# Two graph layers on one core: the first layer's adjacency product by Strassen's scheme, in step with the projection before it, and sums moved to GpSimd at the end

## The chip, the cores and the metric

The kernel runs on one core of one Trainium2 chip. The metric is the device time of one execution in microseconds (us). Before the change its median over 10 runs is 2680.24 us, with single runs between 2676.88 and 2682.38 us.

A core has five engines that each work through a queue of their own: TensorE (PE in the profile; its weight loads are shown apart, as PEld), VectorE (DVE), ScalarE (ACT), GpSimd (POOL) and SyncE (SP, which here only issues transfers). They meet at semaphores.

## The reference

The input x holds 64 batches of 256 tokens with 512 features; adj is one 256 by 256 matrix for all batches. Two layers follow each other, each with a layer norm and a relu ahead and a residual sum behind:

```python
h = relu(layernorm(x))
x = x + (einsum('nm,bmd->bnd', adj, h) @ W0 + b0)          # layer 0
h = relu(layernorm(x))
q, k, v = (h @ W + b for W, b in ...)                       # layer 1: 8 heads of 64
scores = q k^T / 8 + (1 - adj) * -1e9
x = x + (softmax(scores) v) @ Wo + bo
```

All of it is in float32. The change is about the einsum with adj in layer 0, and about the last groups of layer 1.

## The kernel before

**Groups.** The batches are worked in 32 groups of two. The first layer runs over all groups; its results (the residual and the normalised, transposed features, called hidden) go to DRAM and are read again by the second layer, which also runs group by group.

**A group of the first layer** (`ready` at line 678, `layer0` at line 702). A group has four token tiles of 128 tokens. DVE takes the mean and variance of each tile (`moments`, lines 42 and 43), then `norm_scales` (lines 46 to 54) writes rs and nb: two small operations on DVE (lines 51, 52) and two on POOL (lines 53, 54: a power and a product). ACT then writes the normalised relu, h (line 693). TensorE multiplies h as the weights with the transposed adjacency as the moving operand: 16 matmuls of 128 by 128 by 256 (line 714), which leave y transposed, yT, in four PSUM banks that ACT copies to SBUF (line 724). 

**Strassen's scheme** is used already for every projection. `project` (line 456) works a product of 2 by 2 blocks with 7 block products instead of 8, in the form of Winograd. It needs four sums of weight blocks (s1 to s4, made once) and four sums of data blocks (t1 to t4, `Halves.sums`, line 446, on POOL). Each block product is four matmuls of 128 by 128 by 256 (line 453). Partial sums stay in PSUM where they can, and are added to their place in SBUF by DVE (`add`, line 665). Two of the banks start with the bias, copied there by ACT (`seeded`, line 255). The second layer applies the scheme a second time to three of the seven block products (`project2`, line 564, matmuls of 128 by 128 by 128).

Behind the first layer's projection DVE takes the statistics of the new x (lines 761 and 766), `norm_scales` follows for each batch, ACT writes the relu (line 741), DVE transposes it by blocks of 32 (line 747), and SP stores residual (line 751) and hidden (line 756).

**What sets the order.** Nothing is scheduled by a planner: each engine runs its instructions in the order in which the program issues them. The program issues by steps: generators yield after a block product, `tick` (line 271) then advances a clock by one and issues whatever `after(delay, ...)` (line 267) has put off until that step. So the delays in the calls of `ready`, in `relu`, `turn`, `leave_residual` and `leave_hidden`, and in `score` and `attend` set where each instruction stands in its engine's queue. Each group of the first layer is 11 steps: four for the adjacency, seven for the projection. PSUM banks are handed out first in, first out (`bank`, `give`).

**The second layer** has per group and per half of the heads: `score` (line 888: matmuls of line 898, mask by DVE at line 904, a subtraction on POOL at line 910 or on DVE at line 908, the exponential on ACT at line 915, key sums on POOL at line 922), `attend` (line 924: sums of line 931, products with v of line 938, reciprocals on DVE at line 951, the division at line 969), and the projections q, k, v and o. At the division, `HO[g].sums` makes the data sums of the output projection, and `note` (line 963) lets ACT add up the reciprocals for a check of the softmax's range: at the very end a flag is set from these sums (lines 1078 to 1082), and a general path for inputs out of range is run if it is above zero.

Of the kernel before, what the change touches and what calls it, by code (L numbers as in the profile page):

```python
# [8 lines left out]
F32 = mybir.dt.float32  # L9
I32 = mybir.dt.int32  # L10
AF = mybir.ActivationFunctionType
ALU = mybir.AluOpType
# [186 lines left out]
def kernel(  # L199
# [499 lines left out]
                after(scales_at[t // n], scales, t // n)  # L699
            after(relus_at[t], relu, t)  # L700

    def layer0(g):

        xt, h = X.pop(g), H0.pop(g)

        yT = act.tile([P, DC, GN], F32, tag=f"yT{g % 2}", name=f"yT_{g}")
        halves = Halves(f"y_{g}", [yT[:, :, k * N:(k + 1) * N] for k in range(GB)], g % 2 if g < NG - 1 else 0)
        pss = {}

        def adjacency(d, b):  # L710
            if d not in pss:
                pss[d] = bank([P, GN], f"py_{g}_{d}")
            for k in range(NT):
                nc.tensor.matmul(pss[d][:, b * N:(b + 1) * N], h[:, b * NT + k, d * P:(d + 1) * P],  # L714
                                 adjT[:, k, :], start=(b + k == 0), stop=(k == NT - 1), skip_group_check=True)

        if g == 0:
            for d in range(DC):
                adjacency(d, 0)
        for d in range(DC):  # L720
            for b in range(1 if g == 0 else 0, GB):
                adjacency(d, b)
            ps = pss.pop(d)
            nc.scalar.copy(yT[:, d, :], ps)  # L724
            give(ps)
            halves.sums(nc.gpsimd, ("t1",) if d < 2 else ("t2",), d % 2)
            if d == 3:
                halves.sums(nc.gpsimd, ("t3", "t4"))
            if d == 2:
                seeds = seeded(b0_r, f"w_{g}")  # L730
            yield

        mv = small.tile([P, T, 2], F32, tag="mv", name=f"mv1_{g}")
        st = [small.tile([P, 2, nc.vector.BN_STATS_DIM], F32, tag="st1", name=f"st1_{g}_{t}", bufs=8) for t in range(T)]
        h1 = act.tile([P, T, D], F32, tag="h1", name=f"h1_{g}")
        r = act.tile([P, DC * NI, GB, NT, 32], F32, tag="r", name=f"r_{g}")
        done = []

        def relu(k, rs, nb):
            for t in range(NT):  # L740
                nc.scalar.activation(h1[:, k * NT + t, :], xt[:, k * NT + t, :], AF.Relu,  # L741
                                     bias=nb[:, t:t + 1], scale=rs[:, t:t + 1])

        def turn(k):

            for t in range(NT):
                nc.vector.transpose(r[:, :, k, t, :], h1[:, k * NT + t, :].rearrange("p (j b) -> p j b", b=32))

        def leave_residual(k):
            for i in range(NI):  # L750
                nc.sync.dma_start(by_block(X1[g][k], i), blocks_of(xt, i, k))

        def leave_hidden():
            dst = HT[g].rearrange("(j f) d i k n -> i f d j (k n)", f=32)
            for i in range(NI):
                nc.sync.dma_start(dst[i], r[32 * i:32 * i + 32].rearrange("p (d j) k t b -> p d j (k t b)", j=NI))

        def finished(i, k):
            o = quarter(xt, i, k)
            for t in range(NT):  # L760
                nc.vector.bn_stats(st[k * NT + t][:, i, :], o[:, t, :])  # L761
            done.append(k)
            if done.count(k) == 2:
                s = slice(k * NT, (k + 1) * NT)
                for t in range(k * NT, (k + 1) * NT):
                    nc.vector.bn_aggr(mv[:, t, :], st[t])
                rs, nb = norm_scales(nc, small, mhalf, mv[:, s, :], f"1_{g}_{k}")
                wait = 2 if g < NG - 1 else 3
                after(wait, relu, k, rs, nb)
                after(1 if len(done) < 4 else 2, leave_residual, k)  # L770
                after(wait + 1, turn, k)
# [152 lines left out]
    def attend(g, qd):  # L924


        pd = bank([P, GN], f"pden_{g}_{qd}")
        po = [bank([P, GN], f"pav_{g}_{qd}_{f}") for f in range(2)]
        for b in range(GB):
            for h in range(4):  # L930
                nc.tensor.matmul(pd[h * 32:(h + 1) * 32, b * N:(b + 1) * N], ones[:, 0:32], AS[h // 2, b][:, h % 2, :],  # L931
                                 start=(b == 0), stop=True, tile_position=(0, h * 32), skip_group_check=True)
        for b in range(GB):
            v = V[g][qd, b]
            for k in range(NT):
# [12 lines left out]
        give(pd)  # L948

        def invert(c):  # L950
            nc.vector.reciprocal(rden[:, c * P:(c + 1) * P], den[:, c * P:(c + 1) * P])  # L951

        early = 2 if g >= FIRST2 and (g, qd) != (NG - 1, 1) else 4
        for c in range(early):
            invert(c)
        if qd == 0:

            last = g == NG - 1
            OT[g] = (xpool if last else act).tile([P, DC, GN], F32, tag="x" if last else "r", name=f"oT_{g}")
            HO[g] = Halves(f"o_{g}", [OT[g][:, :, k * N:(k + 1) * N] for k in range(GB)], 0 if last else 1)  # L960

        def note():
            nc.scalar.activation(den, rden, AF.Identity, accum_out=stats[:, 1, i:i + 1])

        def divide():
            for c in range(early, 4):
                invert(c)
            for f in range(2):
                nc.vector.tensor_tensor(OT[g][:, 2 * qd + f, :], po[f], rden, op=ALU.mult)
                give(po[f])  # L970
            if g < NG - 1:
                after(3, note)
            else:
                note()
            eng = nc.gpsimd if g < NG - 2 else nc.vector
            if qd == 0:
                HO[g].sums(eng, ("t1",))
            else:
                HO[g].sums(eng, ("t3", "t2", "t4"))
                if g >= FIRST2:  # L980
                    block_outputs(g, eng if g == NG - 1 else nc.gpsimd, 8 if g == NG - 2 else 2)

        after(1, divide)

# [5 lines left out]

    side = [[] for _ in range(NG)]
    mask_steps, bias_steps = masks(), out_bias()
    STEPS = 11
    for i, n in enumerate("qkvo"):
        side[2 + 2 * i].append((load_layer1, n))
        side[4 + 4 * i].append((lambda n: weight_sums(nc.gpsimd, L1[n][0], n, [2 + STEPS * j for j in range(4)]), n))
# [4 lines left out]

    ready(0, (0, 0, 2, 2), (0, 2), (1, 1, 3, 3), batches=2)
    load(1)
    tick()
    turn_adjacency()
    split_bias(b0_r)
    tick()
    weight_sums(nc.vector, w0_sb, "0", (0, 0, 6, 7))
    load(2)
    tick()  # L1010
    tick()
    for g in range(NG):
        for fn, *args in side[g]:
            fn(*args)

        if g == 0:
            ready(1, (1, 2, 3, 4), (5,), (6, 7, 8, 9))
            ready(2, (8, 8, 10, 11), (12,), (16, 17, 18, 19))
        elif g + 2 < NG:
            ready(g + 2, (1, 4, 7, 8), (9,), (16, 17, 18, 19))  # L1020
        if g == NG - 2:
            hidden_sums(0, 1, 2, 12, 16)
        steps = layer0(g)
        run(steps, 4)
        if g + 3 < NG:
            load(g + 3)
        if g == NG - 3:
            load_hidden(0)
        if g == NG - 1:
            load_hidden(1)  # L1030
            break
        run(steps)
    run(queries_keys(0))
    score(0, 0, 12)
    tick()
    run(steps)
    hidden_sums(1, 1, 2, 6, 7)
# [1 line left out]
    for g in range(NG):  # L1039
# [13 lines left out]
        if g + 1 < NG:  # L1053
            run(queries_keys(g + 1))
        else:
            last = post(g - 1, seed_outputs(g - 1))
            run(last, 5)
        attend(g, 1)
        if g + 1 < NG:
            score(g + 1, 0, 5)  # L1060
# [5 lines left out]
            if g + 2 < NG:  # L1066
# [1 line left out]
                if g + 2 >= FIRST2:  # L1068
                    block_hidden(g + 2, 6)
                run(post(g, seeds))  # L1070
    tick()
    run(last)
    last = post(NG - 1, seed_outputs(NG - 1))
    run(last, 6)

    bad = tmp.tile([P, 2 * NG * HQ], F32, tag="u", name="bad")
    worst = small.tile([P, 1], F32, tag="worst", name="worst", bufs=1)
# [41 lines left out]
```

## Time and profile before

| | before |
|---|---|
| median of 10 runs | 2680.24 us |
| the profiled execution | 2678.61 us, span 2676.8 us |
| mean granted TensorE clock | 0.997 |
| PE busy | 2644.3 us |
| PEld busy | 2280.0 us |
| DVE busy | 1858.3 us |
| ACT busy | 964.7 us |
| POOL busy | 1780.2 us |
| HBM | 106.96 MB read, 100.66 MB written |

The span is the time from the first to the last instruction of the profiled execution. "Busy" is the time in which an engine had at least one instruction in work; overlapping instructions count once. In the timelines each line has the start and the length in us, the engine, the line in the program, the operation, output and inputs, shapes, and how many instructions were merged into the line (x8); a bracket at the end tells how long the engine sat idle before it, and what ended that. A float32 matmul of the program leaves two records of PE in the trace. The lines of a window give, for a stretch of time, the busy time of PE, PEld, DVE, ACT and POOL in this order, then the granted clock, the share of the DMA engines and the rate in GB/s.

The first layer fills the first 640 us, the second layer the rest; the last 77 us hold 55.77 us of PE.

### The profile page before, as it was taken

How to read it: one execution, taken by the hardware profiler on the slowest of the kernel's cores; microseconds unless marked ns; L12 is line 12 of the kernel's file. 1: busy time of each engine (PE TensorE's matmuls, PEld its weight loads, DVE VectorE, ACT ScalarE, POOL GpSimd, SP SyncE). 2: the span in 40 equal slices, each digit the busy share in tenths (PEclk: the TensorE clock that was granted, in tenths of full speed). 3: DMA queues.
4: the chain of work that ended last, by engine and by line, in shares of the span. 5: the costliest groups of instructions: out<-in, count | busy, mean ns of one | idle time of the engine just before them, and what ended most of it. 6: DMA issues, size and time to landing. Idle time of an engine off the chain costs nothing. (4 is left out here: it accounts for less than half of the span.)

```text
span 2676.8 us, 50183 instructions
## 1 busy us (share of the span) xinstructions
PE 2644.3 (99%) x19332; PEld 2280.0 (85%) x19332; DVE 1858.3 (69%) x4103; ACT 964.7 (36%) x1875; POOL 1780.2 (67%) x1568
## 2 busy tenths in 40 slices
PE   8999999999999999999999999999999999999997
PEld 7888888888888888888888888888888888888885
DVE  6777777774467766667677676676776666767776
ACT  4444445453333333333333333333333333333331
POOL 3454544444778777777777777777777777777772
PEclk9999999999999999999999999999999999999998
DMA  7776666663122211111111111112221111111110
GB/s 184 187 197 168 156 170 165 171 162 80 47 64 56 57 48 48 48 48 48 48 49 48 48 48 48 48 50 65 68 58 48 48 48 48 49 48 48 48 48 33
DMA packets 281058, 210.93 MB, mean 79 GB/s; under 512 B 145904, under 2 KB 212976, under 8 KB 280816
## 3 DMA queue, kind: packets, MB, share of 16 engines
q1 hardware_dynamic: 280352, 207.15, 29.9%
q8 instruction: 155, 2.54, 0.4%
q14 instruction: 87, 0.71, 0.1%
q10 hardware_dynamic: 464, 0.52, 0.1%
HBM read 106.96 MB, written 100.66 MB: 78 GB/s over the span
## 5 line engine op out<-in xcount | busy, mean ns | idle before, releaser
L910 POOL TENSOR_TENSOR a<-a,top 128x1024 f32<-128x1024 f32 x254 | 592.7, 2367 | 493.5 <-DVE a L904 493.5
L904 DVE SCALAR_TENSOR_TENSOR a<-sc,maskT 128x512 f32<-128x512 f32 x512 | 311.9, 680 | 122.0 <-PE sc L898 122.0
L922 POOL TENSOR_TENSOR as<-a 128x512 f32<-128x512 f32 x256 | 318.9, 1277 | 9.4 <-ACT a L915 8.4
L915 ACT ACTIVATE a<-a 128x1024 f32<-128x1024 f32 x256 | 270.7, 1058 | 10.1 <-POOL a L910 7.7
L53 POOL TENSOR_TENSOR rs<-rs,mhalf 128x2 f32<-128x2 f32 (+1 forms) x97 | 78.4, 808 | 268.0 <-DVE nb L52 267.8
L951 DVE RECIPROCAL rest<-rest 128x128 f32<-128x128 f32 x256 | 224.3, 919 | 34.9 <-ACT rest L947 34.9
L898 PE MATMUL sc<-q,k 64*128 64x256 f32 x2048 | 238.4, 383 | 0.0
L938 PE MATMUL pav<-a,v 128*32 128x256 f32 x4096 | 234.0, 379 | 0.0
L898 PEld LDWEIGHTS sc<-q,k 64*128 64x128 f32 x2048 | 194.2, 187 | 44.7 <-issue 26.3
L714 PE MATMUL py<-adjT,h 128*128 128x256 f32 x1024 | 228.2, 381 | 0.9 <-DVE adjT L333 0.9
L714 PEld LDWEIGHTS py<-adjT,h 128*128 128x128 f32 x1024 | 195.7, 191 | 28.5 <-ACT h L693 1.2
L938 PEld LDWEIGHTS pav<-a,v 128*32 128x32 f32 x4096 | 134.0, 110 | 87.5
L741 ACT ACTIVATE h<-x,nb,rs 128x512 f32<-128x512 f32 x128 | 97.1, 806 | 307.1 <-POOL nb L54 307.1
L947 ACT ACTIVATE rest<-pden 128x512 f32<-128x512 f32 x64 | 38.2, 597 | 414.7 <-PE pden L931 414.7
L665 DVE TENSOR_TENSOR k<-k,k 128x128 f32<-128x128 f32 (+1 forms) x300 | 96.0, 352 | 126.2 <-PE k L564 124.1
L446 POOL TENSOR_TENSOR t_y<-yT 128x256 f32<-128x256 f32 (+1 forms) x96 | 87.6, 913 | 45.1 <-ACT yT L724 41.7
L665 DVE TENSOR_TENSOR x<-o,x 128x128 f32<-128x128 f32 (+1 forms) x360 | 110.9, 349 | 3.1
L665 DVE TENSOR_TENSOR v<-v,v 128x128 f32<-128x128 f32 (+1 forms) x300 | 95.3, 351 | 14.5 <-PE v L564 11.5
L665 DVE TENSOR_TENSOR q<-q,q 128x128 f32<-128x128 f32 (+1 forms) x300 | 96.0, 352 | 13.6 <-PE q L564 11.5
L761 DVE BATCH_NORM_STATS2 st<-x 128x6 f32<-128x256 f32 x256 | 96.4, 418 | 4.4
L693 ACT ACTIVATE h<-x,nb,rs 128x512 f32<-128x512 f32 x128 | 93.9, 805 | 10.2 <-POOL nb L54 10.2
L446 POOL TENSOR_TENSOR t_y<-yT,t_y 128x256 f32<-128x256 f32 (+1 forms) x96 | 87.2, 916 | 13.3 <-ACT yT L724 13.3
(4280 smaller groups left out, 6494.5 us busy)
## 6 DMA issues: line engine op xcount, KB each, us to landing
x<-in_x_dram SPq DMA_DIRECT2D x256, 128.0 KB, 3.3
residual<-x SPq DMA_DIRECT2D x256, 128.0 KB, 2.3
hidden<-r SPq DMA_DIRECT2D x128, 256.0 KB, 4.7
h1T<-hidden SPq DMA_DIRECT2D x64, 512.0 KB, 9.6
x<-residual SPq DMA_DIRECT2D x32, 1024.0 KB, 7.5
out_dram<-x SPq DMA_DIRECT2D x62, 512.0 KB, 4.1
w_sb<-in_L_gnn_weight_dram SPq DMA_DIRECT2D x1, 1024.0 KB, 7.0
wq_sb<-in_L_gnn_Wq_dram SPq DMA_DIRECT2D x1, 1024.0 KB, 7.6
```

Source lines behind the costliest of these rows:

```text
L446: eng.tensor_tensor(self.t[n][:, c, :], self.operand(p, c), self.operand(q, c), op=ALU.subtract)
L665: nc.vector.tensor_tensor(o, ps, u, op=ALU.add)
L714: nc.tensor.matmul(pss[d][:, b * N:(b + 1) * N], h[:, b * NT + k, d * P:(d + 1) * P], adjT[:, k, :], start=(b + k == 0), stop=(k == NT - 1 ...
L741: nc.scalar.activation(h1[:, k * NT + t, :], xt[:, k * NT + t, :], AF.Relu, bias=nb[:, t:t + 1], scale=rs[:, t:t + 1])
L761: nc.vector.bn_stats(st[k * NT + t][:, i, :], o[:, t, :])
L898: nc.tensor.matmul(ps[j][:, kt * N:(kt + 1) * N], k[j * HD:(j + 1) * HD, c, kt * P:(kt + 1) * P], q[j * HD:(j + 1) * HD, c, :], start=(kt ...
L904: nc.vector.scalar_tensor_tensor(a[:, j * NT:(j + 1) * NT, :].rearrange("p k n -> p (k n)"), ps[j], SCALE, maskT_f, op0=ALU.mult, op1=ALU.add)
L910: nc.gpsimd.tensor_tensor(a, a, top_b, op=ALU.subtract)
L915: nc.scalar.activation(a, a, AF.Exp)
L922: nc.gpsimd.tensor_tensor(AS[c, b], a4[:, :, 0, :], a4[:, :, 1, :], op=ALU.add)
L938: nc.tensor.matmul(po[f][h * 32:(h + 1) * 32, b * N:(b + 1) * N], v[:, k, h * HD + f * 32:h * HD + f * 32 + 32], A[h // 2, b][:, (h % 2) * ...
L951: nc.vector.reciprocal(rden[:, c * P:(c + 1) * P], den[:, c * P:(c + 1) * P])
```

## The change

**Adjacency.** For groups 1 to 31 the product with adj is done by Strassen's scheme too, with one level: 7 block products, each of four matmuls of 128 by 128 by 128 (28 per group instead of 16 of twice the width). The blocks of adj are 128 by 128; their four sums are made once, on POOL (`adjacency_sums`). The blocks of h are halves of the features by token tiles; their four sums are made for every group on POOL (`feature_sums`, `last_feature_sum`). Three banks are used: four results are copied to yT by ACT, three are added to it by DVE. Group 0 keeps the old product (`first_adjacency`).

**Order.** The adjacency product of group g + 1 is issued between the block products of group g's projection, so that a group is 7 steps, not 11. The statistics, scales and relus of group g + 2, the sums, the load of group g + 3 and the weight sums get new steps. The last group's projection begins ahead of the second layer's first q and k, with four of its seven block products, and the hidden sums of group 0 stand next to it.

**The end of the kernel.** The data sums of the last two output projections are issued on POOL instead of DVE, those of group 30 seven steps later; the sum of reciprocals of the last group (`note`) is issued two or three steps later; the output projection of group 30 does a sixth of its seven steps ahead of the last attention; the flag is set behind two steps of the last projection instead of six.

```diff
-    def layer0(g):
-        ...
-        def adjacency(d, b):
-            ...
-                nc.tensor.matmul(pss[d][:, b * N:(b + 1) * N], h[:, b * NT + k, d * P:(d + 1) * P],
-                                 adjT[:, k, :], start=(b + k == 0), stop=(k == NT - 1), skip_group_check=True)
-        ...
+    def feature_sums(g):
+
+        def block(i, j):
+            return H0[g].rearrange("p (b j) d -> p b j d", b=GB)[:, :, j - 1, (i - 1) * HF:i * HF]
+        s12 = act.tile([P, 2, GB, HF], F32, tag="t2", name=f"hs12_{g}")
+        s4 = act.tile([P, GB, HF], F32, tag="t24", name=f"hs4_{g}")
+        HS[g] = dict(a11=block(1, 1), a12=block(1, 2), a22=block(2, 2), s1=s12[:, 0], s2=s12[:, 1], s3=block(2, 1), s4=s4)
+        for o, p, q, op in ((s12[:, 0], block(2, 1), block(2, 2), ALU.add), (s12[:, 1], s12[:, 0], block(1, 1), ALU.subtract),
+                            (block(2, 1), block(1, 1), block(2, 1), ALU.subtract)):
+            nc.gpsimd.tensor_tensor(o, p, q, op=op)
+
+    def last_feature_sum(g):
+        nc.gpsimd.tensor_tensor(HS[g]["s4"], HS[g]["a12"], HS[g]["s2"], op=ALU.subtract)
+
+    def adjacency(g):
+        ...
+        def product(ps, a, b, start=True):
+            for c in range(2):
+                for m in range(GB):
+                    nc.tensor.matmul(ps[:, c, m, :], HS[g][a][:, m, c * P:(c + 1) * P], AT[b],
+                                     start=(start and c + m == 0), stop=True, skip_group_check=True)
+        ...
+        pa = new("a")
+        product(pa, "a11", "b11")
+        nc.scalar.copy(place(0, 0), pa)
+        yield
+        pc = new("c")
+        product(pc, "s3", "t3")
+        nc.scalar.copy(place(1, 1), pc)
+        yield
+        product(pa, "s2", "t2", False)
+        nc.scalar.copy(place(1, 0), pa)
+        yield
+        pb = new("b")
+        product(pb, "a12", "b21")
+        more(pb, 0, 0)
+        give(pb)
+        yield
+        product(pa, "s1", "t1", False)
+        more(pa, 1, 1)
+        yield
+        product(pc, "a22", "t4", False)
+        more(pc, 1, 0)
+        give(pc)
+        yield
+        product(pa, "s4", "b22", False)
+        nc.scalar.copy(place(0, 1), pa)
+        give(pa)
+        after(1, YH[g].sums, nc.gpsimd, ("t1", "t2"))
+        after(2, YH[g].sums, nc.gpsimd, ("t3", "t4"))
+        yield
...
-            if g < NG - 1:
-                after(3, note)
-            else:
-                note()
-            eng = nc.gpsimd if g < NG - 2 else nc.vector
-            ...
+            after(2 if (g, qd) == (NG - 1, 1) else 3, note)
+            wait = 7 if (g, qd) == (NG - 2, 1) else 0
+            sums = lambda: HO[g].sums(nc.gpsimd, ("t3", "t2", "t4") if qd else ("t1",))
+            if wait:
+                after(wait, sums)
+            else:
+                sums()
+            if qd and g >= FIRST2:
+                block_outputs(g, nc.gpsimd, wait + 1 if g >= NG - 2 else 2)
...
+    ready(1, (4, 4, 4, 4), (4,), (5, 5, 6, 6))
+    after(6, feature_sums, 1)
+    after(7, last_feature_sum, 1)
...
-        elif g + 2 < NG:
-            ready(g + 2, (1, 4, 7, 8), (9,), (16, 17, 18, 19))
...
+        if g + 2 < NG:
+            ready(g + 2, (1, 1, 2, 2), (2,), (3, 3, 4, 4))
+            after(4, feature_sums, g + 2)
+            after(6, last_feature_sum, g + 2)
+        weighted, turned = layer0(g, seeds), adjacency(g + 1)
+        for i, n in enumerate((0, 0, 0, 1, 1, 2, 3) if g == 0 else (1, 1, 2, 2, 1, 0, 0)):
+            next(weighted)
+            for _ in range(n):
+                next(turned)
+            if i == 5:
+                seeds = seeded(b0_r, f"w_{g + 1}")
+            tick()
+            if i == 3 and g + 3 < NG:
+                load(g + 3)
...
+    hidden_sums(0, 1, 1, 2, 2)
+    steps = layer0(NG - 1, seeds)
+    run(steps, 4)
     run(queries_keys(0))
-    score(0, 0, 12)
+    score(0, 0, 6)
...
-            run(last, 5)
+            run(last, 6)
...
-    tick()
     run(last)
     last = post(NG - 1, seed_outputs(NG - 1))
-    run(last, 6)
+    run(last, 2)
```

More of the change, by code (lines that the diff above doesn't have):

```diff
@@ L700, in ready, with begin_y, first_adjacency, part @@
             after(relus_at[t], relu, t)
-    def layer0(g):
-        xt, h = X.pop(g), H0.pop(g)
-        yT = act.tile([P, DC, GN], F32, tag=f"yT{g % 2}", name=f"yT_{g}")
-        halves = Halves(f"y_{g}", [yT[:, :, k * N:(k + 1) * N] for k in range(GB)], g % 2 if g < NG - 1 else 0)
+    Y, YH, HS, AT = {}, {}, {}, {}
+    def begin_y(g):
+        yT = Y[g] = act.tile([P, DC, GN], F32, tag=f"yT{g % 2}", name=f"yT_{g}")
+        YH[g] = Halves(f"y_{g}", [yT[:, :, k * N:(k + 1) * N] for k in range(GB)], (g + 1) % 2)
+        return yT
+    def first_adjacency():
+        yT, h = begin_y(0), H0.pop(0)
         pss = {}
-        def adjacency(d, b):
+        def part(d, b):
             if d not in pss:
-                pss[d] = bank([P, GN], f"py_{g}_{d}")
+                pss[d] = bank([P, GN], f"py_{d}")
             for k in range(NT):
@@ L715, in adjacency @@
                                  adjT[:, k, :], start=(b + k == 0), stop=(k == NT - 1), skip_group_check=True)
-        if g == 0:
-            for d in range(DC):
-                adjacency(d, 0)
         for d in range(DC):
-            for b in range(1 if g == 0 else 0, GB):
-                adjacency(d, b)
+            part(d, 0)
+        for d in range(DC):
+            part(d, 1)
             ps = pss.pop(d)
@@ L725, in layer0, with adjacency_sums, block @@
             give(ps)
-            halves.sums(nc.gpsimd, ("t1",) if d < 2 else ("t2",), d % 2)
+            YH[0].sums(nc.gpsimd, ("t1",) if d < 2 else ("t2",), d % 2)
             if d == 3:
-                halves.sums(nc.gpsimd, ("t3", "t4"))
-            if d == 2:
-                seeds = seeded(b0_r, f"w_{g}")
+                YH[0].sums(nc.gpsimd, ("t3", "t4"))
             yield
+    def adjacency_sums():
+        def block(j, k):
+            return adjT[:, j - 1, (k - 1) * P:k * P]
+        t = act.tile([P, 4, P], F32, tag="t24o", name="adjT_t")
+        AT.update(b11=block(1, 1), b21=block(2, 1), b22=block(2, 2), t1=t[:, 0, :], t2=t[:, 1, :], t3=t[:, 2, :],
+                  t4=t[:, 3, :])
+        for o, p, q in (("t1", block(1, 2), block(1, 1)), ("t2", block(2, 2), AT["t1"]),
+                        ("t3", block(2, 2), block(1, 2)), ("t4", block(2, 1), AT["t2"])):
+            nc.gpsimd.tensor_tensor(AT[o], p, q, op=ALU.subtract)
@@ new lines, in last_feature_sum, with place, new, more @@
+    def last_feature_sum(g):
+        nc.gpsimd.tensor_tensor(HS[g]["s4"], HS[g]["a12"], HS[g]["s2"], op=ALU.subtract)
+    def adjacency(g):
+        yT = begin_y(g)
+        H0.pop(g)
+        def place(i, k):
+            return yT[:, 2 * i:2 * i + 2, :].rearrange("p c (b k n) -> p c b k n", b=GB, k=NT)[:, :, :, k, :]
+        def product(ps, a, b, start=True):
[3 more added lines that the diff above has]
+                                     start=(start and c + m == 0), stop=True, skip_group_check=True)
+        def new(n):
+            return bank([P, 2, GB, P], f"py_{g}{n}")
+        def more(ps, i, k):
+            o = place(i, k)
+            add(o, ps, o)
+        pa = new("a")
[27 more added lines that the diff above has]
+        yield
@@ L733, in layer0 @@
+    def layer0(g, seeds):
+        xt, halves = X.pop(g), YH.pop(g)
         mv = small.tile([P, T, 2], F32, tag="mv", name=f"mv1_{g}")
@@ L970, in divide @@
                 give(po[f])
-            if g < NG - 1:
-                after(3, note)
-            else:
-                note()
-            eng = nc.gpsimd if g < NG - 2 else nc.vector
-            if qd == 0:
-                HO[g].sums(eng, ("t1",))
-            else:
-                HO[g].sums(eng, ("t3", "t2", "t4"))
-                if g >= FIRST2:
-                    block_outputs(g, eng if g == NG - 1 else nc.gpsimd, 8 if g == NG - 2 else 2)
+            after(2 if (g, qd) == (NG - 1, 1) else 3, note)
[3 more added lines that the diff above has]
+                after(wait, sums)
+            else:
+                sums()
+            if qd and g >= FIRST2:
+                block_outputs(g, nc.gpsimd, wait + 1 if g >= NG - 2 else 2)
         after(1, divide)
@@ L992 @@
     mask_steps, bias_steps = masks(), out_bias()
-    STEPS = 11
+    STEPS = 7
     for i, n in enumerate("qkvo"):
@@ L1003 @@
     load(1)
+    ready(1, (4, 4, 4, 4), (4,), (5, 5, 6, 6))
+    after(6, feature_sums, 1)
+    after(7, last_feature_sum, 1)
     tick()
     turn_adjacency()
+    adjacency_sums()
     split_bias(b0_r)
@@ L1011 @@
     tick()
-    for g in range(NG):
+    steps = first_adjacency()
+    run(steps, 3)
+    seeds = seeded(b0_r, "w_0")
+    run(steps)
+    for g in range(NG - 1):
         for fn, *args in side[g]:
             fn(*args)
-        if g == 0:
-            ready(1, (1, 2, 3, 4), (5,), (6, 7, 8, 9))
-            ready(2, (8, 8, 10, 11), (12,), (16, 17, 18, 19))
-        elif g + 2 < NG:
-            ready(g + 2, (1, 4, 7, 8), (9,), (16, 17, 18, 19))
[L1021 to L1026, printed above, removed]
+        if g + 2 < NG:
[12 more added lines that the diff above has]
+                load(g + 3)
+        for rest in (weighted, turned):
+            for _ in rest:
+                pass
         if g == NG - 3:
             load_hidden(0)
[L1029 to L1032, printed above, removed]
+    load_hidden(1)
+    hidden_sums(0, 1, 1, 2, 2)
+    steps = layer0(NG - 1, seeds)
+    run(steps, 4)
     run(queries_keys(0))
-    score(0, 0, 12)
+    score(0, 0, 6)
     tick()
```

## The prediction

> **What bounds the kernel now.** I read the busy shares first, then one steady group of the first layer as a window, then the timelines of that group and of the end.
>
> ```profile
> PE 2644.3 (99%) x19332; PEld 2280.0 (85%) x19332; DVE 1858.3 (69%) x4103; ACT 964.7 (36%) x1875; POOL 1780.2 (67%) x1568
> 303.59:322.58 18.99, 18.99 (x89) 16.72 (x88) 14.42 (x37) 8.85 (x14) 9.52 (x13) 1.00 0.64 166
> ```
>
> TensorE has no gap in a group (18.99 of 18.99 us); DVE works 14.42 us of it, ACT 8.85, POOL 9.52. So the time is TensorE's work plus what it waits at both ends. The TensorE timeline prices that work: a chain of adjacency matmuls, the projection products after it, and 128-wide matmuls of the second layer.
>
> ```profile
> 303.37 7.07 PE L714 MATMUL py<-adjT,h 128*128 128x256 f32 x32
> 310.28 1.89 PE L453 MATMUL w_15a<-w_sb,yT 128*128 128x256 f32 x8
> 312.00 1.89 PE L453 MATMUL w_15b<-w_sb,yT 128*128 128x256 f32 x8
> ...
> 2576.64 0.38 PE L564 MATMUL q<-t,spare_w_sb 128*128 128x128 f32 x2
> 2576.86 0.39 PE L564 MATMUL q<-t,wq_sb 128*128 128x128 f32 x2
> 2577.08 0.39 PE L564 MATMUL q<-t,spare_w_sb 128*128 128x128 f32 x2
> ```
>
> One program matmul leaves two records. From starts: 16 adjacency matmuls of 256 columns take 310.28 - 303.37 = 6.91 us (0.432 each); a product of four takes 1.72; a 128-wide one takes 0.223, each with its own weights.
>
> The other engines' lines of that group are the hops that I need below:
>
> ```profile
> 320.57 0.16 DVE L52 TENSOR_SCALAR nb<-mv 128x4 f32<-128x4 f32 x1
> 320.74 1.01 POOL L53 TENSOR_TENSOR rs<-rs,mhalf 128x4 f32<-128x4 f32 x1 [5.98 <-DVE nb L52]
> 321.82 0.20 POOL L54 TENSOR_TENSOR nb<-nb,rs 128x4 f32<-128x4 f32 x1
> ...
> 310.96 2.93 ACT L693 ACTIVATE h<-x,nb,rs 128x512 f32<-128x512 f32 x4
> ...
> 312.25 1.28 POOL L446 TENSOR_TENSOR t_y<-yT 128x512 f32<-128x512 f32 x1
> 313.49 1.27 POOL L446 TENSOR_TENSOR t_y<-yT,t_y 128x512 f32<-128x512 f32 x1
> ...
> 304.93 1.52 ACT L741 ACTIVATE h<-x,nb,rs 128x512 f32<-128x512 f32 x2 [10.03 <-POOL nb L54]
> 305.91 1.30 DVE L747 STREAM_TRANSPOSE r<-h 128x512 f32<-128x512 f32 x2
> 307.14 0.65 DVE L42 BATCH_NORM_STATS2 st<-x 128x6 f32<-128x512 f32 x1
> ```
>
> POOL idles 5.98 us here, and one 512-element sum on it takes 1.24 us from start to start. Last, TensorE's waits at the end:
>
> ```profile
> 2612.16 0.49 PE L564 MATMUL v<-spare_w_s,t 128*128 128x128 f32 x2 [3.86 <-DVE v L665]
> 2632.51 3.78 PE L453 MATMUL o_30a<-wo_sb,oT 128*128 128x256 f32 x8 [5.41 <-ACT o_30a L255]
> 2653.02 0.49 PE L564 MATMUL o<-spare_w_s,rest 128*128 128x128 f32 x2 [2.04 <-DVE x L665]
> 2667.95 0.19 PE L1081 MATMUL pf<-ones,worst 128*1 128x1 f32 x2 [1.96 <-DVE worst L1079]
> ```
>
> **What the Trainium skill says.** "TensorE: Matmul & The Clock Gate", section "Architectural detail": TensorE can pull weight loads ahead of running matmuls, while ACT and DVE are strict first-in first-out queues and GpSimd is too per core. The trace agrees on the first (a new weight every 0.223 us without a gap); the second is what my argument rests on. The same page, "What's actually happening": after about 3.4 us of idling the matmul clock halves. The trace shows it: after the 5.41 us wait a product takes about 3.6 us, not 1.72. "GPSIMD Engine Reference", section 3.1: a two-input sum is 1.96 times slower on GpSimd than on VectorE; here 1.27 against 0.69 us, 1.8 times.
>
> **The change, part by part.**
>
> *TensorE in the first layer.* For 31 groups 16 matmuls of 0.432 us (6.91) become 28 of 0.223 (6.25): 0.66 us less per group, 20.4 in all. The floor of a group is 7 x 1.727 + 6.25 = 18.34 us.
>
> *DVE.* Three sums from PSUM are new per group, about 0.61 us start to start beside others: 14.42 + 1.8 = 16.3 us. It still fits in 18.34.
>
> *POOL.* Four 512-element feature sums are new, 4 x 1.24 = 5.0: 9.5 + 5.0 = 14.5 us. This fits too. ACT's four copies per group stay.
>
> *But the order closes a ring.* Let T be the end of DVE's nb for the features of group g+2. In each queue's new order:
> 1. POOL rs and nb: 322.02 - 320.74 = 1.28.
> 2. ACT, four relus: 2.93 (the first feature sum reads all four token tiles); hops 0.12.
> 3. POOL, in its order: s1, s2, s3 of g+2 (1.36, as s2 needs s1, 1.24, 1.24), t1, t2 of the next yT (1.36, 1.24), rs/nb of the finished batch 0 (0.97), s4 (1.24), t3, t4 (2.48), rs/nb of batch 1 (0.97): 12.1.
> 4. ACT relu of batch 1 to the end of DVE's two transposes of it: 307.14 - 304.93 = 2.21, hop 0.04.
> 5. DVE: behind those transposes the last two token tiles of group g+3, two times 0.78, then rs, nb: 1.9. That nb is the next T.
>
> Sum: 1.28 + 3.05 + 12.1 + 2.25 + 1.9 = 20.6 us. No engine is full, yet every hop waits for the one before through a queue or true data, and there is one ring per group. In the kernel before, rs/nb of both batches went to POOL ahead of long sums (it idled 5.98 us), so no such ring bound. The period becomes 20.6, not 18.34: against 19.05 before ((596.03 - 310.28)/15, the first products of groups 30 and 15), 1.55 us more.
>
> Where TensorE stands in that period: ACT's copy of the third adjacency product is behind the relu of batch 1, so the fifth product waits 1.6 us for it; the fifth projection product waits some 0.5 us for DVE's add behind nb. Both are shorter than an idle that halves the clock for sure; if it halved, the ring has 2 us to hide it. A second path in the ring (transposes of batch 0, two tiles, an add and its statistics) comes 0.4 us earlier.
>
> *First groups.* ACT's order now puts group 1's relus, which wait for its x, between the copies of group 0's yT. The x tiles' statistics end at about 19.5 us, POOL's rs/nb at 20.8, relus, copies and seed at 25.6: the first product starts there, not at 21.16, and POOL's t2, behind three feature sums, holds the third until 31. Walking the queues, T of group 2 is at 33.8 and of group 3 at 56.7.
>
> *End of the layer.* T of group 31: 56.7 + 28 x 20.58 = 632.9. Group 30's first product follows 7.0 later, 639.9 (596.03 before). Group 30 has one ring wait left: 18.34 + 1.65, so group 31 starts at 659.9; four products bring q of group 0 to 666.8. The same amount of TensorE work was done before at 615.02 + 6.91 = 621.9: +44.9. Then 10 products, not 14, lie between the first score and its attention; the last key sum ends about 0.7 us after TensorE arrives: +0.7.
>
> *SP.* The load of x moves to the fourth of seven steps; its 8 issues follow 4 hidden stores (3.8 us) and take 5.5: landing some 10.7 us after T, needed at 14. In the four groups with a weight load (7 us) this cover goes: +2 together. Below the cover a gain is excluded.
>
> *The end of the kernel.* The 3.86 us wait goes when the sums of the second last group leave DVE, with the slow clock behind it (about 2). The seeds no longer wait behind the sum of reciprocals (L963 sat behind DVE's division): of 5.41 some 3 are saved, as the first add still waits for DVE. But the sums now come on POOL: the last attention's key sums stand behind them, about 3 us back, and t3 of the last group costs another 2.2. Flag: 1.96 becomes about 1.5. The inner step fills part of the wait, and 2.04 goes. Net -7 (bounds -11, +1 if POOL holds every product).
>
> Sum on the profiled execution (2678.61, span 2676.8): +44.9 + 0.7 + 2 - 7 = +40.6, so 2719.2; the median lies 1.6 above it: 2721.
>
> **The rivals.**
> - *TensorE stays the bound* (faster). It needs a ring of 18.34 or less: I would have to be 2.3 us over in 20.6, for instance if relus and sums overlap by token tile. Then -20.4 + 5 (start) - 7 = -22: 2658. For it: POOL and DVE have time. Against: s1 reads all four tiles, and POOL's order is fixed. 0.10.
> - *A longer ring.* If POOL's seven long sums take 0.2 us more each beside a busier DVE (a 128x512 one took 1.72 at 2632.97), the period is 22.0: 28 x 1.4 = +39, 2760. A late x would do the same. 0.15.
> - *Weight loads bind the 128-wide matmuls.* A load record lasts 0.19 us; if loads ran singly, 56 x 0.191 = 10.7 and a group 22.8: 31 x 3.8 + 1.7 - 7 = +112, 2793. Against: the 0.223 us spacing above. 0.04.
> - *Part of the ring overlaps*, period 18.9 to 19.8, 2673 to 2699. 0.05.
>
> **How the numbers follow.** The ring as summed has 0.66; its own range is 20.0 to 21.2 us, 28 x 0.6 = 17 either way, so 2703 to 2739. To hold 8 in 10 I add the upper part of the partial overlap and most of the longer ring: 2690 to 2770, which leaves out 0.10 + 0.03 + 0.04 + 0.03 = 0.20. About 0.2% (5 us) is what a measurement here can tell from no change: the faster rival and a little of the overlap give 0.11, within 0.03, slower 0.86.
>
> **What would show it.** Right: in the first layer groups start about 20.6 us apart; TensorE is some 90% busy there, with gaps ahead of the fifth adjacency product (ended by ACT's copy) and of the fifth projection product (ended by DVE's add); no engine is full; the layer's end is 45 us later; layer two's steady groups stay equal. Wrong: a period near 18.3 without gaps, or adjacency matmuls more than 0.23 us apart at full clock, or gaps ended by DMA.

## The result, and the profile after

The changed kernel takes 2721.85 us (median of 8 runs, 2718.26 to 2723.19); the kernel before, in 28 runs beside it, 2680.15 us. The ratio is 1.0155, with a 95% interval of 1.0146 to 1.0164: 41.7 us slower. The forecast was 2721.

The busy shares of the changed kernel, and behind them a window of one group of the first layer (columns: length, then PE, PEld, DVE, ACT, POOL busy, clock, DMA share, GB/s):

```profile
PE 2643.7 (97%) x20076; PEld 2280.9 (84%) x20076; DVE 1941.2 (71%) x4182; ACT 966.1 (36%) x1875; POOL 1938.1 (71%) x1648
```

```profile
419.00:439.50 20.50, 18.92 (x114) 16.68 (x113) 17.52 (x41) 8.87 (x14) 14.06 (x16) 1.00 0.57 154
```

A group lasts 20.5 us, and TensorE is busy in 18.92 of them; before, it was busy in 18.99 of 18.99. No other engine is full: DVE works 17.5 us, POOL 14.1. The TensorE timeline of that group shows where it waits:

```profile
429.77 1.16 PE L770 MATMUL py_20a<-adjT_t,hs 128*128 128x128 f32 x8 [1.32 <-ACT yT L789]
...
432.09 1.99 PE L453 MATMUL w_19a<-w_s,t_y 128*128 128x256 f32 x8 [0.27 <-DVE x L665]
...
440.06 1.05 PE L770 MATMUL py_21a<-adjT,h 128*128 128x128 f32 x8
440.95 1.89 PE L453 MATMUL w_20b<-w_sb,yT 128*128 128x256 f32 x8
```

These are the two places that the forecast named: the fifth adjacency product, for ACT's copy of the third (1.32 us), and the fifth projection product, for DVE's add (0.27 us). A block product of four narrow matmuls takes 0.89 us (440.06 to 440.95), four times 0.223.

What TensorE waits for is the ring. Its hops in the timelines of DVE, POOL and ACT, from one nb of the features to the next:

```profile
349.06 0.16 DVE L52 TENSOR_SCALAR nb<-mv 128x4 f32<-128x4 f32 x1
349.24 1.01 POOL L53 TENSOR_TENSOR rs<-rs,mhalf 128x4 f32<-128x4 f32 x1 [3.00 <-DVE nb L52]
...
350.56 2.93 ACT L693 ACTIVATE h<-x,nb,rs 128x512 f32<-128x512 f32 x4 [3.05 <-POOL nb L54]
...
353.56 1.27 POOL L754 TENSOR_TENSOR hs<-h 128x512 f32<-128x512 f32 x1 [3.04 <-ACT h L693]
...
365.36 0.20 POOL L54 TENSOR_TENSOR nb<-nb,rs 128x2 f32<-128x2 f32 x1
...
365.59 1.52 ACT L821 ACTIVATE h<-x,nb,rs 128x512 f32<-128x512 f32 x2 [2.63 <-POOL nb L54]
366.44 1.42 DVE L827 STREAM_TRANSPOSE r<-h 128x512 f32<-128x512 f32 x2 [0.25 <-ACT h L821]
...
369.62 0.16 DVE L52 TENSOR_SCALAR nb<-mv 128x4 f32<-128x4 f32 x1
```

The reader is to follow the brackets: each line idles until the one above it is done, and the last line is the first again, 20.56 us later. From end to end: rs and nb on POOL 1.30; relus 3.04; POOL from the first feature sum to the nb of batch 1 12.00 (353.56 to 365.56, with no idle time); relu and transposes 2.30; the two tiles with their rs and nb 1.92. Sum 20.56; the forecast had 1.28, 3.05, 12.1, 2.25, 1.9.

The tail of TensorE, where it still waits:

```profile
2663.48 0.41 PE L1011 MATMUL pden<-as,ones 128*32 128x256 f32 x2 [1.00 <-POOL as L1002]
2677.34 2.98 PE L453 MATMUL o_30a<-wo_s,t_o 128*128 128x256 f32 x8 [2.32 <-DVE x L665]
2687.53 0.64 PE L1011 MATMUL pden<-as,ones 128*32 128x256 f32 x8 [1.61 <-POOL as L1002]
...
2700.16 1.99 PE L453 MATMUL o_31c<-wo_sb,t_o 128*128 128x256 f32 x8 [1.91 <-POOL t_o L446]
2704.45 0.19 PE L1172 MATMUL pf<-ones,worst 128*1 128x1 f32 x2 [2.29 <-DVE worst L1170]
```

The waits of 3.86 us (v) and 5.41 us (seeds) are gone; new ones stand behind POOL's sums, and one of 2.32 us behind an add of DVE.

Where the time came from, read as the first start of the same work in the two profiled executions:

| | before | after | difference |
|---|---|---|---|
| first projection product (group 0) | 21.2 | 27.4 | +6.2 |
| first projection product of group 1 | 40.8 | 50.4 | +9.6 |
| of group 30 | 596.0 | 644.0 | +48.0 |
| same amount of work done as at q of group 0 | 621.9 | 671.0 | +49.1 |
| q of group 1 | 675.9 | 725.8 | +49.9 |
| q of group 31 | 2568.3 | 2618.1 | +49.8 |
| end | 2676.8 | 2721.3 | +44.5 |

The start costs 10 us, the ring 38, the second layer's steady part nothing, and the end gives 5 back.

### The profile page after: what moved, and what is told of

It is laid out like the page before. It is cut to its first block, busy times and chain, and to the rows that moved or that the text cites. A ratio compares the mean times of both kernels' runs of the same rounds, so it can differ in the third digit from the quotient of the medians.

```text
span 2721.3 us, 51869 instructions
## 1 busy us (share of the span) xinstructions
PE 2643.7 (97%) x20076; PEld 2280.9 (84%) x20076; DVE 1941.2 (71%) x4182; ACT 966.1 (36%) x1875; POOL 1938.1 (71%) x1648
## 3 DMA queue, kind: packets, MB, share of 16 engines
q8 instruction: 161, 2.64, 0.4%
## 5 line engine op out<-in xcount | busy, mean ns | idle before, releaser
L827 DVE STREAM_TRANSPOSE r<-h 128x512 f32<-128x512 f32 x128 | 89.9, 709 | 36.0 <-ACT h L821 34.9
L754 POOL TENSOR_TENSOR hs<-h 128x512 f32<-128x512 f32 x31 | 39.4, 1272 | 97.4 <-ACT h L693 88.9
L665 DVE TENSOR_TENSOR q<-q,q 128x128 f32<-128x128 f32 (+1 forms) x300 | 96.0, 352 | 14.1 <-PE q L564 12.0
L446 POOL TENSOR_TENSOR t_o<-oT 128x512 f32<-128x512 f32 x64 | 82.3, 1285 | 10.1 <-DVE oT L1049 10.1
L42 DVE BATCH_NORM_STATS2 st<-x 128x6 f32<-128x512 f32 x128 | 84.2, 658 | 7.2 <-DMA x<-in_x_dram 7.2
```

What stands on the lines that cost most here:

```text
L665: nc.vector.tensor_tensor(o, ps, u, op=ALU.add)
```

## The experiments

The theory: the period of a group is the ring above, and TensorE, DVE and POOL have time to spare in it. Rivals: more TensorE time per narrow matmul than the spacing shows; an engine (POOL, DVE) that is full; the new order of the steps as such.

**Work in the ring, and the same work beside it.** The fourth feature sum is done twice, once at its place and once two steps later, where POOL idles. In both, the second sum only repeats the first.

```diff
             after(6, last_feature_sum, g + 2)
+            after(6, last_feature_sum, g + 2)     # e2; after(8, ...) in e3
```

> The sum s4 of the features is made twice in a row, at its old place in POOL's queue, which lies in the ring. The result is the same. Ring: one more hop of 1.24 us, the period rises from 20.55 to 21.8 us; 28 by 1.24 = 35, about 2757 us. Rival (TensorE or DVE bound in the first layer): 2722 us, as POOL has some 6 us to spare in a group.

> The same second s4, but issued two steps later, where POOL waits for DVE's nb (3.0 us idle in the changed kernel), outside the ring. Ring: no change, 2722 us within 3. Rival (POOL's amount of work counts): as with the sum in the ring, about 2757 us.

In the ring: 2762.24 us, ratio 1.0306 (1.0288 to 1.0323), 40.4 us more than the changed kernel. Beside it: 2721.22 us, ratio 1.0155 (1.0139 to 1.0172), no more. The timeline of POOL shows the size of the first:

```profile
381.45 2.63 POOL L757 TENSOR_TENSOR hs<-h,hs 128x512 f32<-128x512 f32 x2
```

Two sums into one tile take 2.63 us, one 1.27, so each of 30 groups gets 1.36 more: 40.8. It comes through one to one. The same sum, the same load on POOL, out of the ring costs nothing: POOL is not full.

**TensorE's own time.** The fourth adjacency product is issued twice (its second pass starts the bank anew, so it only repeats).

```diff
         product(pb, "a12", "b21")
+        product(pb, "a12", "b21")
         more(pb, 0, 0)
```

> The fourth adjacency product of each group is worked twice by TensorE (the second overwrites the first, so the result is the same): 0.89 us more TensorE work in each of 31 groups. Ring: TensorE waits about 1.6 us a group in the changed kernel, so nearly all of it is hidden: 2722 to 2727 us. Rival (TensorE bounds the group): 31 by 0.89 = 28, about 2749 us.

2723.22 us, ratio 1.0162 (1.0145 to 1.0179). Of 0.89 us more per group nothing is left in the period (20.5 to 20.6), because the wait behind it shrinks by as much: 1.32 us before the fifth product above, and here

```profile
430.44 1.16 PE L770 MATMUL py_20a<-adjT_t,hs 128*128 128x128 f32 x8 [0.42 <-ACT yT L789]
```

TensorE is not the bound of the changed kernel.

**A shorter ring, and one that I missed.** The four sums of yT go two steps later, out of the way of batch 1's rs and nb (group 1 keeps its places).

```diff
-        after(1, YH[g].sums, nc.gpsimd, ("t1", "t2"))
-        after(2, YH[g].sums, nc.gpsimd, ("t3", "t4"))
+        after(1 if g == 1 else 3, YH[g].sums, nc.gpsimd, ("t1", "t2"))
+        after(2 if g == 1 else 4, YH[g].sums, nc.gpsimd, ("t3", "t4"))
```

> The four data sums t1 to t4 of yT are issued two steps later, so that on POOL they stand behind rs/nb of both batches, not between them. No work is added or left out. Ring: it loses the four sums (5.0 us) and falls from 20.55 to about 15.5 us a group, so TensorE's 18.3 to 18.5 us bounds; 28 groups by 2.1 us less than the changed kernel's 2721.9, about 2662 us, and the waits of TensorE for ACT's copy and for DVE's add go. Rival (128-wide matmuls, or the three DVE sums, cost more than their lines show): the same work is there, 2722 us. Rival (POOL is simply too full): 2722 us.

2704.14 us, ratio 1.0088 (1.0071 to 1.0105): faster by 17.7 than the changed kernel, but not 2662. Most groups are 19.7 us apart. TensorE now waits elsewhere, and POOL shows why:

```profile
354.05 1.99 PE L453 MATMUL w_16a<-w_s,t_y 128*128 128x256 f32 x8 [1.06 <-POOL t_y L446]
```

```profile
350.44 0.70 POOL L53 TENSOR_TENSOR rs<-rs,mhalf 128x2 f32<-128x2 f32 x1
351.22 0.20 POOL L54 TENSOR_TENSOR nb<-nb,rs 128x2 f32<-128x2 f32 x1
351.37 1.28 POOL L446 TENSOR_TENSOR t_y<-yT 128x512 f32<-128x512 f32 x1
352.73 1.27 POOL L446 TENSOR_TENSOR t_y<-yT,t_y 128x512 f32<-128x512 f32 x1
```

I had cut one ring and closed another. t2, which the third projection product of group g + 1 needs, now stands behind rs and nb of batch 1 of group g, and these need the last projection product of group g. From the third product to the end of the last of one group is 13.4 us on TensorE; DVE's add, statistics, aggregate, rs and nb take 2.65; POOL's rs, nb, t1, t2 take 3.6: 19.65 us. One of the two rings had to be seen before the other was cut.

**Both rings opened.** Only one step later for the sums of yT, so that t1, t2 stand between the two rs/nb, and the fourth feature sum behind them all.

```diff
-        after(1, YH[g].sums, nc.gpsimd, ("t1", "t2"))
-        after(2, YH[g].sums, nc.gpsimd, ("t3", "t4"))
+        after(1 if g == 1 else 2, YH[g].sums, nc.gpsimd, ("t1", "t2"))
+        after(2 if g == 1 else 3, YH[g].sums, nc.gpsimd, ("t3", "t4"))
...
-            after(6, last_feature_sum, g + 2)
+            after(8, last_feature_sum, g + 2)
```

> The changed kernel with another order of POOL's queue in the first layer: the four sums of yT (t1 to t4) one step later and the last feature sum s4 behind them, so that neither a long sum of the next group stands ahead of the statistics of batch 1 nor t1, t2 behind them by more than they need; group 1 keeps the old places. Ring theory: between two nb of the features POOL now holds only rs/nb 1.28, s1 to s3 3.9, rs/nb 0.97, t1, t2 2.5 and rs/nb 0.97; with the relus 3.05 and DVE's 2.25 + 1.9 the ring is 16.9 us, below TensorE's 18.34, so TensorE sets the period again at 18.4 to 18.6: from the 2704.1 us of the run with t1 to t4 moved alone (period 19.65), 28 x 1.2 less = about 2669, and the third projection product shows no wait for POOL. Rival, the 28 narrow matmuls or DVE's three adds set the period: 2700 or more. Rival, a new ring through t3, t4 or s4 (the seventh product waits for s4): a period of 19 to 20, 2685 to 2710, with a wait for POOL ahead of one product in each group.

2669.79 us, ratio 0.9963 (0.9949 to 0.9976). The same instructions as in the changed kernel, 52 us less. The groups are 18.3 to 18.5 us apart, and a line of POOL's timeline shows that the ring has slack now: POOL idles before the nb of the features comes.

```profile
341.36 1.02 POOL L53 TENSOR_TENSOR rs<-rs,mhalf 128x4 f32<-128x4 f32 x1 [0.79 <-DVE nb L52]
```

Eight groups (13, and 20 to 26) stay longer. The first, 22.3 us, holds the matmuls of the output bias (line 400), as it does in the kernel before (22.4). In the others (18.6 to 20.1 us) DVE gets more work, the masks made from adj: it is busy 16.9 to 18.4 us a group, against 16.24 in a steady one. In the slice below it is busy 17.81 us, and the wait of TensorE at the slice's end has DVE's name. The seven cost 4.2 us together, of which 0.65 is TensorE's own work on the masks (lines 349 and 366).

```profile
484.00:503.50 19.50, 19.07 (x115) 17.04 (x115) 17.81 (x43) 8.96 (x14) 13.72 (x17) 1.00 0.66 179
```

```profile
503.51 1.97 PE L453 MATMUL w_25a<-w_s,t_y 128*128 128x256 f32 x8 [0.38 <-DVE x L665]
```

**The start undone too.** The relus of group 1 go behind ACT's copies of group 0's yT.

```diff
-    ready(1, (4, 4, 4, 4), (4,), (5, 5, 6, 6))
-    after(6, feature_sums, 1)
-    after(7, last_feature_sum, 1)
+    ready(1, (4, 4, 4, 4), (4,), (8, 8, 8, 8))
+    after(9, feature_sums, 1)
+    after(10, last_feature_sum, 1)
```

> The same order of POOL, and the start undone: the relus of group 1 stand behind ACT's copies of group 0's yT instead of between them, and its feature sums later on POOL. If the start lost about 6 us by that order of ACT (first product at 27.4 against 21.2) and some 3 more by the halved clock after that idle time, the first product comes at about 21.3 and the time is 6 to 9 us below the kernel with the order alone: about 2661. If the late weights (a wait of 1.5 us on a DMA was seen there) or the feature sums of group 1 set the first groups, at most 3 us come back: 2666 or more.

2662.52 us, ratio 0.9935 (0.9921 to 0.9949), 7.3 us less. The start of the changed kernel and of this one, in TensorE's timeline:

```profile
27.40 3.78 PE L453 MATMUL w_0a<-w_sb,yT 128*128 128x256 f32 x8 [6.58 <-ACT w_0a L255]
30.97 2.80 PE L453 MATMUL w_0b<-w_sb,yT 128*128 128x256 f32 x8
33.61 1.89 PE L453 MATMUL w_0a<-w_s,t_y 128*128 128x256 f32 x8
```

```profile
21.99 1.99 PE L453 MATMUL w_0a<-w_sb,yT 128*128 128x256 f32 x8 [0.30 <-ACT w_0a L255]
23.82 1.89 PE L453 MATMUL w_0b<-w_sb,yT 128*128 128x256 f32 x8
25.55 1.89 PE L453 MATMUL w_0a<-w_s,t_y 128*128 128x256 f32 x8
```

The wait of 6.58 us goes, and with it two slow products (3.57 and 2.64 us from start to start, against 1.83 and 1.73). In this kernel a steady group is TensorE's alone: the first products of groups 14 to 20 start 18.34 us apart, which is the floor that the forecast worked out, and TensorE has no gap:

```profile
328.70:347.00 18.30, 18.30 (x114) 16.85 (x113) 16.24 (x41) 8.99 (x14) 13.97 (x15) 1.00 0.66 178
```

DVE (16.24) and POOL (13.97) work about as much as the sums of the forecast said (16.3 and 14.5), and do not bind.

**The steps without Strassen's product.** The plain product of 16 matmuls in the new seven steps, without the feature sums, the sums of adj's blocks and DVE's adds.

```diff
-        pa = new("a")
-        product(pa, "a11", "b11")
-        ...
+        for d in range(DC):
+            ps = bank([P, GN], f"py_{g}_{d}")
+            for b in range(GB):
+                for k in range(NT):
+                    nc.tensor.matmul(ps[:, b * N:(b + 1) * N], h[:, b * NT + k, d * P:(d + 1) * P],
+                                     adjT[:, k, :], start=(b + k == 0), stop=(k == NT - 1), skip_group_check=True)
+            nc.scalar.copy(yT[:, d, :], ps)
+            give(ps)
```

> The changed kernel with the adjacency product of groups 1 to 31 done plainly, by 16 matmuls of 256 columns and four copies, in the same seven steps; no feature sums, no sums of the adjacency's blocks, no DVE adds out of PSUM. Loads, relus, statistics and the end stay as changed. Ring theory: without the 5 us of feature sums on POOL the ring is about 15.6 us, TensorE sets the period at 19.0, and what is left over the kernel before is the start (+6 to +9) less the end (-5): 2680 to 2686. Rival, the new order of the steps itself (later loads of x, relus after the statistics, sums one step later) costs the time: a period of 20 or more, 2710 or more.

2678.17 us (2676.09 to 2682.65), ratio 0.9995 (0.9987 to 1.0003): as the kernel before, and 2 us under the range expected. The period is 19.0. So the order of the steps does not lengthen the period; it takes the feature sums to close the ring. (The run also leaves out the three adds and the narrow products; that these do not set the period is shown by the runs with POOL reordered and with a product done twice.) Against this kernel the one with POOL reordered is 8.4 us faster by the medians and 12.7 by the two profiled executions; that of the plain product is 4.3 us slower than its own median. So Strassen's product gives 8 to 13 us of the 20.4 that TensorE's arithmetic promises. In the two profiled executions some 4 us go in the groups where DVE is busier, 1.4 in group 0 (23.0 us to the first product of group 1, against 21.7) and 1.3 in groups that last up to 18.5 us instead of 18.34. What takes the rest is not known.

**The end alone.** The kernel before with the edits of the end only.

```diff
-            eng = nc.gpsimd if g < NG - 2 else nc.vector
-            ...
+            after(2 if (g, qd) == (NG - 1, 1) else 3, note)
+            wait = 7 if (g, qd) == (NG - 2, 1) else 0
+            sums = lambda: HO[g].sums(nc.gpsimd, ("t3", "t2", "t4") if qd else ("t1",))
+            ...
-            run(last, 5)
+            run(last, 6)
...
-    tick()
     run(last)
...
-    run(last, 6)
+    run(last, 2)
```

> The kernel before with the edits of the end alone: the sums of the last two output projections on POOL, the sums of reciprocals and the flag later, an inner step ahead of the last attention. The first layer is as before. From the two traces the end gained 5.3 us after the score of the last group: about 2675. My forecast was -7 (2673). If the gain needed the first layer's changes, or if POOL's sums give it all back, 2678 to 2681.

2671.52 us, ratio 0.9969 (0.9957 to 0.9981): 9.0 us less by the medians, more than the 5.3 expected. By the profiled executions 7.4 (2676.8 to 2669.4), of which 0.5 lie ahead of q of group 31. The edits of the end are a gain by themselves.

**The last sums back on DVE.** In the kernel with order and start mended, the sums t3, t2, t4 of the very last output projection go to DVE again.

```diff
-            sums = lambda: HO[g].sums(nc.gpsimd, ("t3", "t2", "t4") if qd else ("t1",))
+            eng = nc.vector if (g, qd) == (NG - 1, 1) else nc.gpsimd
+            sums = lambda: HO[g].sums(eng, ("t3", "t2", "t4") if qd else ("t1",))
```

> The kernel with POOL reordered and the start undone, and in it one edit of the end undone too: the sums t3, t2, t4 of the very last output projection on DVE again. There the trace had a wait of 1.92 us on POOL's sum ahead of o_31c, and after it a halved clock (a product in 2.81 us for 1.73). My step said that t3 on POOL costs 2.2 us. If so, the wait falls to 1.2 or less and with it the slow clock: 1 to 4 us below that kernel, 2658 to 2661. If DVE, which has adds from PSUM and the flag's statistics to do at that point, makes TensorE wait as long behind them, the time is the same or up to 2 us longer: 2662 to 2664, and the wait has DVE's name.

2662.10 us, ratio 0.9933 (0.9919 to 0.9946): no difference from 2662.52. TensorE waits a little less for the sum and a little more for the flag:

```profile
2640.68 1.97 PE L453 MATMUL o_31c<-wo_sb,t_o 128*128 128x256 f32 x8 [1.39 <-DVE t_o L446]
2645.15 0.19 PE L1173 MATMUL pf<-ones,worst 128*1 128x1 f32 x2 [2.51 <-DVE worst L1171]
```

The 1.92 us on POOL became 1.39 on DVE, and 2.29 became 2.51, since the flag's two operations now stand behind the sums. The slow product (o_31a, 2.81 us before and 3.24 here) that I had put down to the first wait stands behind the second, the flag's. Which engine does these sums makes no difference that these runs can tell.

## Why the prediction was right

**The ring: right, in place and size.** Its five hops sum to 20.56 us in the trace, 20.6 in the forecast, and the groups start 20.5 to 20.6 us apart. Work put into it comes out one to one (40.4 us for 40.8), work put beside it is free, and opening it takes 52 us off. The rival "TensorE stays the bound" fell for want of overlap, as argued: s1 starts 0.07 us after the last relu. But its figure was the right one for another order of the same queue: with the ring open the period is 18.3.

**TensorE, DVE and POOL per group: right.** The floor of 18.34 us and the two loads show in the kernel with the ring open. Weight loads do not bind: a narrow product takes 0.89 us with the ring closed and open.

**The start: right in mechanism, its cost too small.** The forecast put the first product at 25.6. In the profiled execution it came at 27.40, because a load of weights landed later there (DVE's line 422 waits 1.54 us for it, and the statistics of group 1's x stand behind it); in the run with the sum beside the ring, whose start is the same code, it came at 25.58. What the step left out is the clock. It let TensorE idle for 4 to 6 us and then priced the next products at full speed. The first took 3.57 us instead of 1.73 (3.49 in the other run), and DVE's first add waits for its end:

```profile
31.29 0.69 DVE L665 TENSOR_TENSOR x<-w_0a,x 128x512 f32<-128x512 f32 x1 [9.48 <-PE w_0a L453]
```

From this add DVE works without a wait up to the nb of group 2's features, which ends at 37.6 instead of the 33.8 forecast: 1.8 us of it for the late load, 1.8 for the slow product. (In the other run, without the late load, it ends at 35.8.) The second product was slow too, 2.64 us, but the third could hardly have begun sooner: POOL's t2 for it ended at 33.35, and it began at 33.61. (In the other run it began at 30.80; the forecast was 31.) I had quoted "TensorE: Matmul & The Clock Gate", section "What's actually happening", on idling for the waits at the end, and did not apply it here, where the trace agrees with it. Together the first layer's end came at +49.1, not +44.9; 3.9 of these 4.2 were there by the nb of group 3's features (60.6 instead of 56.7).

**Weight loads beside a late x, +2: not there.** In the changed kernel the groups 20 to 26 take 144.0 us, and seven times 20.55 is 143.9. The groups that do grow when the ring is open have DVE's name on their waits, not DMA's. The step named the wrong resource, and the ring hid the right one. It hid the matmuls of the output bias likewise: group 13 and the two behind it take 24.0, 18.3 and 19.7 us, 62.0 together, against 61.7 for three rings.

**Layer two and its first key sum:** +0.7 forecast, +0.8 measured.

**The end: -7 forecast, -5.3 measured** in this profile, and -6.9 with the edits alone (from q of group 31 to the end 101.6 us, 108.5 before). Up to the first output projection of group 30 the tail gains 11 us (2632.5 to 2671.3, at +49.8 before it), and gives 5.7 back from there to the end, in which TensorE waits for an add of DVE (2.32 us), for POOL's key sums (1.61 and 0.59), for POOL's last sum (1.91) and for the flag. Forecast was that the flag's wait falls to 1.5; it grew to 2.29. Of the 1.6 us between the two, 1.0 is the clock: after the wait of 2.3 us o_30a takes 2.98 us here and 1.97 with the end alone.

The sum was 40.6 and came out at 44.5 in the profiled execution (2721.3 against 2676.8): 4.2 from the start, 0.1 from the key sums, -2 from the weight loads, 1.6 from the end. The medians lie 41.7 apart. The forecast put the median of the changed kernel 1.6 us above its profiled execution, as in the kernel before; it lies 1.2 below. That executions differ by when that first load lands is shown only by the two profiles with the same start (27.40 and 25.58); for the other executions it is assumed. So it is partly luck that the median was forecast to within 1 us: the profiled execution came 3.9 us later than forecast, with the start 4.2 and the end 1.6 dearer than forecast and the weight loads 2 cheaper, and the step from there to the median came 2.8 us the other way.

**Where I was wrong after the prediction:** the run with the sums of yT moved two steps, expected at 2662, gave 2704. The step that failed was to recompute one ring and take the rest as slack.

## What to carry to other kernels

Where several engines with queues in program order serve each other in a loop over groups, add up each closed path from an instruction to its own next occurrence, through data and through queue places; the longest of these is the period, even if no engine is full. When a new operation is put into such a loop, ask of each queue what stands behind it, and after cutting one ring sum up the others before trusting the gain. Here the same instructions took 2721.9 us in one order of a queue and 2669.8 in another, and 2662.5 with the first group's order mended as well, 0.65% below the kernel before.

## What was not expected

- With the fourth sum doubled in the ring, the groups are not evenly long: of 16 in a row most alternate between about 20.9 and 23.0 us. The mean rises by the added time all the same. In the stretch from 360 to 448 us the two short groups have waits of 1.89 and 2.68 us for ACT's copy, slow products behind them (2.39 and 2.92 us) and a granted clock of 0.92; the two long ones have waits of 1.65 us and a clock of 1.00. Why they alternate was not tried.
- TensorE slows after shorter waits than the Trainium skill says ("TensorE: Matmul & The Clock Gate", "What's actually happening": about 3.4 us of idling). A product that takes 1.89 us in these timelines took 2.98 behind a wait of 2.32 us (o_30a above), and o_31a took 2.81 to 3.24 behind the flag's wait of 2.29 to 2.51 in four kernels. But with the same waits o_30a took 1.96 or 1.97 in three other kernels, and o_31a 1.99 in the one with POOL reordered, so the length of the wait alone does not decide, and what does was not tried.
- A ring slower than TensorE swallows TensorE work. The matmuls of the output bias lengthen group 13 by 3.4 us in the kernel before (22.4 for 19.0), and three groups of the changed one by 0.3 together.
